# Graph layers on one core: the first group's preparation, weight sums and stage order rearranged

## The chip, the cores and the metric

The kernel runs on one core of a Trainium2 chip. The metric is the device time of one execution in microseconds (us), the median of several; smaller is better. A core has TensorE (PE in the profile, with PEld its weight loads), VectorE (DVE), ScalarE (ACT), GpSimd (POOL) and SyncE (SP, which here only issues DMAs). Each engine runs its own queue in order and waits on semaphores.

## The reference, cut to what matters

128 graphs of 64 nodes, 512 features each, go through four layers; each adds its input and is followed by a normalisation over the features (in the kernel `layer_norm`, without gain and offset).

```python
# layer 0, hypergraph convolution twice (H = adj != 0, w = first row of adj)
D = where(H @ w > 0, 1 / (H @ w), 0);  B = where(H.sum(0) > 0, 1 / H.sum(0), 0)
conv(x, W, b) = D * (H @ (B * (H.T @ (x @ W.T)))) + b
x = norm(x + conv(layer_norm(relu(conv(x, W1, b1)), gamma, beta), W2, b2) + x)
# layer 1: s = x @ w @ a; A = exp(leaky(8 tanh((s_i + s_j) / 8))) * adj, rows scaled to adj's row sums
x = norm(x + (A @ x) @ w)
# layer 2: three graph convolutions, relu after the first two
x = norm(x + adj @ (relu(adj @ (relu(adj @ x @ gW1 + gb1)) @ gW2 + gb2)) @ gW3 + gb3)
# layer 3: attention of 8 heads of 64, softmax mixed with exp(-adj) and adj, then Wout
x = norm(x + attention(x) @ Wout + bout)
```

## The kernel before, in words

All is float32. The 128 graphs are cut into 16 groups of 8 graphs (`T` = 512 rows, four tiles of 128 rows with two graphs each). A group passes through `first_half` (layers 0 and 1; stages named `a.`), `second_half` up to `dots` (layer 2, queries, keys, scores; `b.`), and the rest of it (softmax, values, output; `t.`). In one step of the main loop group q is in `a`, group q-1 in `b`, group q-2 in `t`. A string `order` in the code interleaves their stages; since PE runs its queue in order, a stage of one group fills PE while another group's stage waits for DVE or ACT. In step 0 there is only `a` of group 0, and nothing to fill with. The Tile framework's scheduler sets the final order of each engine's queue from the program's order and its own estimates; `tc.issue_after(i)` keeps what is emitted under it behind instruction i.

**Products.** `multiply` makes a 512x512x512 product from seven products of halves (`product`, L391) instead of eight: the left operand needs four sums on DVE (`Left.sums`, L370 to L373: s1 to s4), the right one four sums t1 to t4 of the weight's quarters. The seven products are called B11, T1, T2, B21, T3, B22, T4 in the order in which PE takes them; each is 8 records of 128x256 in the profile (16 for w2, whose left side has two halves). B11, T2, T3 and T4 build up in one PSUM tile, which is snapped in between (u1 after B11, u2 after T2), so the next of them waits for the eviction; T1 and B22 share another (u5 after T1). Graph products (`graph_T`, L340) use 64x64 matrices. All stages' PSUM copies are on ACT or DVE.

**Weights.** `Stream` keeps a ring of 20 tiles of 256 KB. A weight's first use loads its quarters, and `Weight.make` (L200 to L222) makes t1 to t4 on DVE when the stage takes it (L209 to L212) and writes them to HBM through SP (L218); later groups load all seven parts. W2 is first scaled by gamma on DVE (L207), and `beta_times` (L224) makes bw = beta @ W2.T on PE (L232) from w2's tiles, after c2 of group 0.

**Prepare.** `prepare` (L452 to L502) reads adj twice, by columns (`atc`) and by rows (`adn`), and its first row spread over the partitions (`wb`). It makes ht, hn (the two 0/1 matrices), hn*wb, the row sums deg, D and rowsum, B from ht; `inv` holds 1/D and 1/B, and through dg, hb, rbps (L486) and sps (L498) comes the matrix smat = H' B H D' (L501) that both graph products of layer 0 use. cs = inv * deg goes into the residual with bw (`constant`, L650).

**Order of group 0.** `prepare`, c1 (graph product of x with smat), w1a and w1b (the halves of W1), lnh (relu, LayerNorm of h), c2a and c2b (graph product of h), bw, w2 and the norm of x, then wa = w @ a (`make_wa`, L284: DVE products, sums, one matmul L299), s = x . wa (xwa, L605), e (L609), ss (L613: sums s over PE), t (tanh, exp, times atc), den (L626), its reciprocal rd (L631), c3 (graph product, L340), the l1 product with w, and the norm. `load` and `prep` of the next group stand behind a.c2b and b.k1. `prepare_masks` (L505) loads the masks and makes neg and adt at the end of stage agg.

Of the kernel before, what the change touches and what calls it, by code (L numbers as in the profile page):

```python
# [14 lines left out]
P = 128  # L15
# [25 lines left out]
def kernel(  # L41
# [61 lines left out]

    def load_group(q):


        g0 = q * 2 * G
        atc = grp.tile([P, G, C], FP, name=f"atc_{q}", tag="atc", bufs=3)
        nc.sync.dma_start(out=atc, in_=adjT[g0 : g0 + 2 * G].rearrange("(p g) e i -> (g e) p i", g=2))
        adn = grp.tile([P, G, C], FP, name=f"adn_{q}", tag="adn", bufs=2)  # L110
        nc.sync.dma_start(out=adn, in_=adj[g0 : g0 + 2 * G].rearrange("(p g) i e -> (g i) p e", g=2))
        wb = grp.tile([P, G, C], FP, name=f"wb_{q}", tag="wb", bufs=1)
        for h in range(2):
            nc.sync.dma_start(
                out=wb[h * C : (h + 1) * C],
                in_=adj[g0 : g0 + 2 * G, 0, :].rearrange("(p g) e -> g p e", g=2)[h].partition_broadcast(C),
            )
        xg = xp.tile([P, G, D], FP, name=f"x_{q}", tag="x")
        nc.sync.dma_start(
            out=xg, in_=x[q * T : (q + 1) * T, :].rearrange("(p t) d -> t p d", t=P)  # L120
        )
        atx = grp.tile([P, 2, C], FP, name=f"atx_{q}", tag="atx", bufs=3)
        for h in range(2):
            nc.sync.dma_start(
                out=atx[h * C : (h + 1) * C],
                in_=adjT[g0 : g0 + 2 * G].rearrange("(a z) e i -> z e a i", z=4)[1 + h],
            )
        return dict(q=q, atc=atc, atx=atx, adn=adn, wb=wb, x=xg)
# [37 lines left out]
    class Weight:  # L166
# [30 lines left out]
        def make(self, quads):  # L197

            got = [[None] * self.halves for _ in range(7)]
            if self.scaled:  # L200
                beta_times(quads)
            for u, b in enumerate(quads):
                if self.scaled:
                    for (k, n), t in b.items():
                        c0 = (u * 2 + k) * 2
                        g2 = ga_col[:, c0 : c0 + 2].unsqueeze(2).to_broadcast([P, 2, Q])
                        nc.vector.tensor_mul(t, t, g2)  # L207
                t1, t2, t3, t4 = (self.tile(f"t{n}", 0, u) for n in range(1, 5))
                nc.vector.tensor_sub(t1, b[0, 1], b[0, 0])  # L209
                nc.vector.tensor_sub(t2, b[1, 1], t1)  # L210
                nc.vector.tensor_sub(t3, b[1, 1], b[0, 1])
                nc.vector.tensor_sub(t4, b[1, 0], t2)  # L212
# [3 lines left out]
                for what, t in (whole | made if self.scaled else made).items():  # L216
                    kept[what] = dram.tile([P, 2, Q], FP, name=f"{self.name}k{what}_{u}", tag=f"{self.name}k{what}_{u}")
                    nc.sync.dma_start(out=kept[what], in_=t)  # L218
                self.kept.append(kept)
                for what, t in (whole | made).items():  # L220
                    got[what][u] = t
            return got  # L222

    def beta_times(quads):  # L224

        bb = sp.tile([P, DH // P, P], FP, name="bb", tag="s")
        nc.vector.tensor_copy(bb, be_col.unsqueeze(2).to_broadcast([P, DH // P, P]))
        ps = ps_gt.tile([P, 2, Q], FP, name="bwps", tag="gt")
        for n in range(2):
            for c in range(DH // P):  # L230
                u, k, kc = c // 4, c // 2 % 2, c % 2
                nc.tensor.matmul(  # L232
                    ps[:, n, :], bb[:, c, :], quads[u][k, n][:, kc, :],
                    start=(c == 0 and n == 0), stop=(c == DH // P - 1), skip_group_check=True,
                )
        nc.scalar.copy(bw_bc, ps.rearrange("p n f -> p (n f)"))
# [8 lines left out]
    class Stream:  # L245
# [12 lines left out]
        def pump(self):  # L258
            while self.todo and self.held + self.todo[0][3] <= RING:
                wt, q, what, n = self.todo.pop(0)  # L260
                if q == 0:
                    got = wt.load_quads()
                else:
                    got = [wt.load(q, what, u) for u in range(wt.halves)]
                self.here[wt, q, what] = got
                self.held += n

        def take(self, wt, q, what):
# [3 lines left out]
            if (wt, q, None) in self.here:  # L272
                self.here[wt, q] = wt.make(self.here.pop((wt, q, None)))
# [10 lines left out]
    def make_wa():  # L284

        a_bc = work.tile([P, D], FP, name="a_bc", tag="w")
        nc.gpsimd.dma_start(out=a_bc, in_=a.partition_broadcast(P))
        wa_col = small.tile([P, KD], FP, name="wa_col", tag="wa_col", bufs=1)
        for c in range(KD):
            wr = work.tile([P, D], FP, name=f"wr_{c}", tag="w")  # L290
            nc.sync.dma_start(out=wr, in_=w[c * P : (c + 1) * P, :])
            prod = work.tile([P, D], FP, name=f"waprod_{c}", tag="w")
            nc.vector.tensor_mul(prod, wr, a_bc)
            nc.vector.reduce_sum(wa_col[:, c : c + 1], prod, axis=AX.X)
        dg = work.tile([P, KD, P], FP, name="wa_diag", tag="w")
        for c in range(KD):
            nc.vector.tensor_scalar_mul(dg[:, c, :], ident, wa_col[:, c : c + 1])
        ps = ps_gt.tile([P, D], FP, name="wa_ps", tag="gt")
# [99 lines left out]
    def multiply(lefts, wt_q, dst, key, flipped=False, res=None, before=None, stops=(3,)):  # L398
# [14 lines left out]
        if before is not None:  # L413
            before()
# [37 lines left out]
    def prepare(g):  # L452
        q, atc, adn, wb = g["q"], g["atc"], g["adn"], g["wb"]

        ht = grp.tile([P, G, C], FP, name=f"ht_{q}", tag="ht", bufs=1)
        nc.vector.tensor_scalar(ht, atc, 0.0, None, ALU.not_equal)
        hn = grp.tile([P, 2, G, C], FP, name=f"hn_{q}", tag="hn", bufs=1)
# [507 lines left out]
```

## Time and profile before

| | us |
|---|---|
| median of 3 runs | 2870.9 (2870.55 to 2875.74) |
| the profiled execution | 2871.8 |
| its span (first to last instruction) | 2869.9 |
| PE busy in the span | 2773.6 (97%) |
| DVE busy | 2042.4 (71%) |
| ACT busy | 811.7 (28%) |
| POOL busy | 7.9 |

The profile is of one execution. Its page gives each engine's busy time, 40 slices of the span, DMA queues, the chain of work that ended last, and the costliest groups of instructions. Asked in detail, the trace gives the busy time by stretches of time, the waits (who waited for whom, total us, times, longest us), and a timeline (start us, duration us, engine, line, operation, out<-in). Durations of pipelined matmuls overlap: products of 8 records show 1.89 us and follow each other every 1.725 us.

### The profile page before, as it was taken

How to read it: one execution, taken by the hardware profiler on the slowest of the kernel's cores; microseconds unless marked ns; L12 is line 12 of the kernel's file. 1: busy time of each engine (PE TensorE's matmuls, PEld its weight loads, DVE VectorE, ACT ScalarE, POOL GpSimd, SP SyncE). 2: the span in 40 equal slices, each digit the busy share in tenths (PEclk: the TensorE clock that was granted, in tenths of full speed). 3: DMA queues.
4: the chain of work that ended last, by engine and by line, in shares of the span. 5: the costliest groups of instructions: out<-in, count | busy, mean ns of one | idle time of the engine just before them, and what ended most of it. 6: DMA issues, size and time to landing. Idle time of an engine off the chain costs nothing.

```text
span 2869.9 us, 67654 instructions
## 1 busy us (share of the span) xinstructions
PE 2773.6 (97%) x28802; PEld 2361.6 (82%) x28802; DVE 2042.4 (71%) x3933; ACT 811.7 (28%) x1444; POOL 7.9 (0%) x17
## 2 busy tenths in 40 slices
PE   5799999999999999999999999999999999999998
PEld 4677888888888888888888888888888888888876
DVE  6677767677686776867677686776767677676756
ACT  2132232323223232232323232232223323232222
POOL 1000000000000000000000000000000000000000
PEclk8899999999999999999999999999999999999999
DMA  6444545454454544545455454544545445454441
GB/s 187 162 125 122 152 128 166 127 156 141 131 167 130 161 128 136 165 126 162 127 147 153 128 163 132 156 127 136 166 129 154 128 139 156 126 162 130 146 119 63
DMA packets 313627, 406.05 MB, mean 141 GB/s; under 512 B 57936, under 2 KB 185456, under 8 KB 313328
## 3 DMA queue, kind: packets, MB, share of 16 engines
q1 hardware_dynamic: 312672, 400.13, 46.8%
q8 instruction: 228, 3.74, 0.5%
q0 software_dynamic: 656, 1.60, 0.2%
q14 instruction: 71, 0.58, 0.1%
HBM read 370.70 MB, written 30.93 MB: 140 GB/s over the span
## 4 chain that ended last, share of the span: by engine, by line
PE 80%; DVE 8%; ACT 3%; issue 0%; DVEq 0%; ACTq 0%
PE a_l0w L391 14%; PE b_l0w L391 7%; PE a_v L391 4%; PE a_k L391 4%; PE a_l2b L391 4%; PE a_l2c L391 4%; PE a_q L391 4%; PE a_l2a L391 4%; PE c_l0w L391 4%; PE a_wo L391 3%; PE gt_l L340 3%; PE gt_l0h L340 2%; PE a_l1w L391 2%; PE b_v L391 2%; PE b_k L391 2%; PE b_l2c L391 2%
## 5 line engine op out<-in xcount | busy, mean ns | idle before, releaser
L322 DVE BATCH_NORM_STATS2 st_l<-x 128x6 f32<-128x512 f32 x256 | 165.2, 672 | 0.6
L391 PE MATMUL a_l0w<-w2w,aT_l0h 128*128 128x256 f32 x720 | 164.3, 381 | 0.0
L391 PEld LDWEIGHTS a_l0w<-w2w,aT_l0h 128*128 128x128 f32 x720 | 135.6, 190 | 18.8
L562 ACT ACTIVATE h<-h 128x1024 f32<-128x1024 f32 x64 | 67.7, 1057 | 263.4 <-DVE h L432 239.2
L313 ACT ACTIVATE rs_l<-mv_l,eps_t 128x4 f32<-128x4 f32 x64 | 19.1, 298 | 373.9 <-DVE mv_l L323 373.9
L326 DVE TENSOR_SCALAR x<-x,mv_l,rs_l 128x512 f32<-128x512 f32 x256 | 122.5, 542 | 2.2
L348 ACT COPY aT_l<-gt_l 128x512 f32<-128x512 f32 x192 | 99.1, 598 | 86.9 <-PE gt_l L340 86.8
L391 PE MATMUL b_l0w<-w2w,s_l0h 128*128 128x256 f32 x480 | 108.5, 379 | 0.0
L391 PEld LDWEIGHTS b_l0w<-w2w,s_l0h 128*128 128x128 f32 x480 | 91.2, 190 | 12.4
L391 PE MATMUL a_wo<-wow,aT_oT 128*128 128x256 f32 x360 | 86.7, 384 | 8.5 <-DVE x L428 8.5
L698 ACT ACTIVATE aT_h<-gth,gb_col 128x256 f32<-128x256 f32 x128 | 48.5, 490 | 159.0 <-PE gth L690 159.0
L391 PE MATMUL a_l2b<-gwbw,aT_h 128*128 128x256 f32 x360 | 86.9, 384 | 4.7 <-ACT aT_oT L869 4.7
L408 DVE TENSOR_TENSOR u_l0w<-a_l0w,b_bc 128x512 f32<-128x512 f32 x64 | 43.9, 686 | 64.4 <-PE a_l0w L391 64.4
L391 PE MATMUL a_l1w<-ww,aT_l 128*128 128x256 f32 x360 | 86.9, 384 | 1.6
L391 PE MATMUL a_l0w<-w1aw,aT_l 128*128 128x256 f32 x360 | 88.2, 388 | 0.0
L391 PE MATMUL a_l2a<-aT_l,gwaw 128*128 128x256 f32 x360 | 86.6, 383 | 1.0 <-ACT aT_l L348 1.0
L391 PE MATMUL a_l0w<-w1bw,aT_l 128*128 128x256 f32 x360 | 87.3, 379 | 0.0
L391 PE MATMUL a_v<-wvw,aT_xT 128*128 128x256 f32 x360 | 86.6, 383 | 0.0
L391 PEld LDWEIGHTS a_wo<-wow,aT_oT 128*128 128x128 f32 x360 | 67.1, 190 | 23.0 <-DVE x L428 14.2
L391 PE MATMUL a_l2c<-gwcw,aT_h 128*128 128x256 f32 x360 | 86.0, 382 | 0.0
L391 PE MATMUL a_q<-aT_xT,wqw 128*128 128x256 f32 x360 | 85.1, 379 | 0.5 <-ACT aT_xT L737 0.5
L391 PE MATMUL a_k<-aT_xT,wkw 128*128 128x256 f32 x360 | 85.0, 379 | 0.0
(455 smaller groups left out, 6416.6 us busy)
## 6 DMA issues: line engine op xcount, KB each, us to landing
w2w<-w2k SPq DMA_DIRECT2D x210, 256.0 KB, 2.7
x<-in_x_dram SPq DMA_DIRECT2D x16, 1024.0 KB, 6.3
out_dram<-x SPq DMA_DIRECT2D x16, 1024.0 KB, 4.8
w1aw<-w1ak SPq DMA_DIRECT2D x60, 256.0 KB, 2.8
w1bw<-w1bk SPq DMA_DIRECT2D x60, 256.0 KB, 2.7
ww<-wk SPq DMA_DIRECT2D x60, 256.0 KB, 2.7
gwaw<-gwak SPq DMA_DIRECT2D x60, 256.0 KB, 3.8
gwbw<-gwbk SPq DMA_DIRECT2D x60, 256.0 KB, 2.7
```

What stands on the lines that cost most here:

```text
L313: nc.scalar.activation(rs, mv[:, :, 1], AF.Sqrt, bias=eps_t)
L322: nc.vector.bn_stats(st, xg[:, p, :])
L326: nc.vector.tensor_scalar(xg[:, p, :], xg[:, p, :], mv[:, p, 0:1], rs[:, p : p + 1], ALU.subtract, ALU.mult)
L340: nc.tensor.matmul(ps[g][f * C : (f + 1) * C, c, p, :], src(2 * duo + p)[rows, c0 : c0 + C], mat[rows, 2 * duo + p, :], start=True, stop=True,
L348: nc.scalar.copy(o[:, :, :, g, :], ps[g])
L391: nc.tensor.matmul(acc[:, blk, :], lhsT, rhs, start=(first and blk == 0 and i == 0), stop=(last and i == n_k - 1), skip_group_check=True,)
L408: nc.vector.tensor_add(t, ps, res(m, n))
L562: nc.scalar.activation(hn, hn, AF.Relu)
L698: nc.scalar.activation(o[:, :, h, :], ps[h][:, c].rearrange("p (d a) i -> p d (a i)", d=2), AF.Relu, bias=gb2_col[:, k : k + 1],)
```

## The change

- **Prepare of group 0.** D comes from 8 pairs of 64x64-by-64x1 products on PE (ht times the first column of atc) instead of adn, wb and DVE sums, and is copied from PSUM. `wb` is not loaded for group 0, deg and rowsum are made later. `prepare` becomes a generator in three parts: row work on DVE ("rows"), the rest ("prep"), for group 0 also the row sums.
- **Loads at the start.** x of group 0 in two halves, one on ACT's queue, ahead of adn; atx and masks of all groups with the group's loads (masks before: at agg); W2's raw quarters, w's rows, and all of group 1's inputs early.
- **Weights.** t1 to t4 of w1a stay on DVE; those of w1b, w2, w, gW1 to gW3, Wq, Wk, Wv and Wout are made on GpSimd, as soon as the ring lets them be loaded, and all writes to HBM are issued by GpSimd. W2 is loaded raw into two tiles of `big`, scaled by gamma on ACT into two others. bw is made from the raw tiles.
- **wa.** Its rows are loaded early, products and sums are one DVE operation per row block; its DVE part is emitted during w1b, its matmul behind bw's.
- **Order.** A string `start` is walked first, with each stage's PE work kept in turn: bw and wa between lnh and c2a; rows, prep and c1 of group 1 inside group 0's w2; group 1's w1a from w2's end to den, its residual, and its w1b and lnh behind the l1 product. The main order follows from step 1 without what is done, with "rows" for the next group behind a.w2 and "prep" where it was.
- **VectorE.** The residual of group 0 (2x + b2 and the bw term, `residual`) is emitted in turn behind lnh; later groups' rows behind w2's last add but one; `prepare_masks` behind the l2b product, with gb3.

In the built program the sequence of PE's stages in groups 2 to 15 is that of before. DVE's queue there differs in two places: the 11 kinds of row operations (ht, db, hn, rowsum, deg, hn*wb, db, gt, inv, dg, hb, cs) stand between w2's adds and t instead of beside the k product, and the five mask operations stand between gb3's adds and the eight sums for w2. Of GpSimd's 44 sums the program has four for each of nine weights and eight for w2.

```diff
+    def in_turn(*engines):
+        stack = ExitStack()
+        for e in engines:
+            stack.enter_context(tc.issue_after(
+                next(i for i in reversed(nc.cur_bb.bb.instructions) if i.engine == e)
+            ))
+        return stack
...
     def load_group(q):
...
+        xg = xp.tile([P, G, D], FP, name=f"x_{q}", tag="x")
+        xsrc = x[q * T : (q + 1) * T, :].rearrange("(p t) d -> t p d", t=P)
+        if q == 0:
+            nc.scalar.dma_start(out=xg[:, 0:2], in_=xsrc[:, 0:2])
         atc = grp.tile([P, G, C], FP, name=f"atc_{q}", tag="atc", bufs=3)
         nc.sync.dma_start(out=atc, in_=adjT[g0 : g0 + 2 * G].rearrange("(p g) e i -> (g e) p i", g=2))
+        if q == 0:
+            nc.sync.dma_start(out=xg[:, 2:4], in_=xsrc[:, 2:4])
         adn = grp.tile([P, G, C], FP, name=f"adn_{q}", tag="adn", bufs=2)
...
-        def make(self, quads):
+        def make(self, quads, engine):
...
-            if self.scaled:
-                beta_times(quads)
+            to_keep = []
             for u, b in enumerate(quads):
-                if self.scaled:
-                    for (k, n), t in b.items():
...
+                engine.tensor_sub(t1, b[0, 1], b[0, 0])
+                engine.tensor_sub(t2, b[1, 1], t1)
+                engine.tensor_sub(t3, b[1, 1], b[0, 1])
+                engine.tensor_sub(t4, b[1, 0], t2)
...
+            with in_turn(POOL):
+                for k, t in to_keep:
+                    nc.gpsimd.dma_start(out=k, in_=t)
             return got
...
+        def load_raw(self):
+            self.raw = []
+            for u in range(self.halves):
+                t = big.tile([P, 4, 2, Q], FP, name=f"{self.name}r_{u}", tag="big")
+                for n, (k, m) in enumerate(((0, 0), (0, 1), (1, 1), (1, 0))):
+                    nc.sync.dma_start(out=t[:, n], in_=self.quad_src(u, k, m))
+                self.raw.append(t)
+        def scale(self):
+            quads = []
+            for u, raw in enumerate(self.raw):
+                s = big.tile([P, 4, 2, Q], FP, name=f"{self.name}s_{u}", tag="big")
+                b = {}
+                for n, (k, m) in enumerate(((0, 0), (0, 1), (1, 1), (1, 0))):
+                    for c in range(2):
+                        f = (u * 2 + k) * 2 + c
+                        nc.scalar.mul(s[:, n, c], raw[:, n, c], ga_col[:, f : f + 1])
+                    b[k, m] = s[:, n]
+                quads.append(b)
+            return quads
+        def beta_times(self):
+            bb = sp.tile([P, DH // P, P], FP, name="bb", tag="s")
+            nc.gpsimd.tensor_copy(bb, be_col.unsqueeze(2).to_broadcast([P, DH // P, P]))
+            ps = ps_gt.tile([P, 2, Q], FP, name="bwps", tag="gt")
+            for n in range(2):
+                for c in range(DH // P):
+                    u, k, kc = c // 4, c // 2 % 2, c % 2
+                    nc.tensor.matmul(
+                        ps[:, n, :], bb[:, c, :], self.raw[u][:, ((0, 1), (3, 2))[k][n], kc, :],
+                        start=(c == 0 and n == 0), stop=(c == DH // P - 1), skip_group_check=True,
+                    )
+            nc.scalar.copy(bw_bc, ps.rearrange("p n f -> p (n f)"))
...
         def pump(self):
             while self.todo and self.held + self.todo[0][3] <= RING:
                 wt, q, what, n = self.todo.pop(0)
-                if q == 0:
-                    got = wt.load_quads()
+                self.held += n
+                if q > 0:
+                    self.here[wt, q, what] = [wt.load(q, what, u) for u in range(wt.halves)]
+                elif wt is w_1[0]:
+                    quads = wt.load_quads()
+                    with in_turn(DVE):
+                        self.here[wt, q] = wt.make(quads, nc.vector)
                 else:
-                    got = [wt.load(q, what, u) for u in range(wt.halves)]
-                self.here[wt, q, what] = got
-                self.held += n
+                    self.here[wt, q] = wt.make(wt.scale() if wt.scaled else wt.load_quads(), nc.gpsimd)
...
+    def make_wa(a_bc, wr):
         wa_col = small.tile([P, KD], FP, name="wa_col", tag="wa_col", bufs=1)
         for c in range(KD):
-            wr = work.tile([P, D], FP, name=f"wr_{c}", tag="w")
-            nc.sync.dma_start(out=wr, in_=w[c * P : (c + 1) * P, :])
-            prod = work.tile([P, D], FP, name=f"waprod_{c}", tag="w")
-            nc.vector.tensor_mul(prod, wr, a_bc)
-            nc.vector.reduce_sum(wa_col[:, c : c + 1], prod, axis=AX.X)
+            nc.vector.scalar_tensor_tensor(
+                wr[c], wr[c], 1.0, a_bc, ALU.mult, ALU.mult, accum_out=wa_col[:, c : c + 1]
+            )
         dg = work.tile([P, KD, P], FP, name="wa_diag", tag="w")
         for c in range(KD):
             nc.vector.tensor_scalar_mul(dg[:, c, :], ident, wa_col[:, c : c + 1])
+        return dg
+    def spread_wa(dg):
...
     def prepare(g):
-        q, atc, adn, wb = g["q"], g["atc"], g["adn"], g["wb"]
+        q, atc, adn = g["q"], g["atc"], g["adn"]
...
+        def by_rows():
+            nc.vector.tensor_scalar(hn[:, 0], adn, 0.0, None, ALU.not_equal)
+            nc.vector.reduce_sum(deg, hn[:, 0], axis=AX.X)
+            nc.vector.reduce_sum(rowsum, adn, axis=AX.X)
+        if q == 0:
+            d_ps = [ps_gt.tile([P, G], FP, name=f"dps_{q}_{h}", tag="gt") for h in range(2)]
+            for p in range(G):
+                for h in range(2):
+                    rows = slice(h * C, (h + 1) * C)
+                    nc.tensor.matmul(
+                        d_ps[h][rows, p : p + 1], ht[rows, p, :], atc[rows, p, 0:1], start=True, stop=True
+                    )
+            for h in range(2):
+                rows = slice(h * C, (h + 1) * C)
+                nc.vector.tensor_copy(db[rows, 0], d_ps[h][rows])
+        else:
+            by_rows()
+            nc.vector.tensor_mul(hn[:, 1], hn[:, 0], g["wb"])
+            nc.vector.reduce_sum(db[:, 0], hn[:, 1], axis=AX.X)
...
         nc.vector.tensor_mul(hb, ht, bcast(inv[:, 1], G))
+        yield
...
+        if q == 0:
+            yield
+            by_rows()
+        nc.vector.tensor_mul(cs, inv[:, 0], deg)
+        yield
...
-                with behind(f"l0w10_{q}"):
-                    for p in range(G):
-                        nc.vector.scalar_tensor_tensor(xg[:, p, :], xg[:, p, :], 2.0, b2_bc, ALU.mult, ALU.add)
-                    if q > 0:
-                        constant(g)
+                if q > 0:
+                    with behind(f"l0w10_{q}"):
+                        residual(g)
                 yield "resid"
...
+        if q == 0:
+            with in_turn(DVE):
+                residual(g)
         for left in lefts:
             left.sums()
         yield "c2b"
-        gen = multiply(lefts, (w_2, q), nat(xg), f"l0w2_{q}", res=nat(xg), before=(lambda: constant(g)) if q == 0 else None)
...
-    def constant(g):
+    def residual(g):
         for p in range(G):
+            nc.vector.scalar_tensor_tensor(
+                g["x"][:, p, :], g["x"][:, p, :], 2.0, b2_bc, ALU.mult, ALU.add
+            )
             nc.vector.scalar_tensor_tensor(
                 g["x"][:, p, :], bw_bc, g["cs"][:, p : p + 1], g["x"][:, p, :], ALU.mult, ALU.add
             )
...
         with behind(f"l2b_{q}"):
             for p in range(G):
                 nc.vector.tensor_add(xg[:, p, :], xg[:, p, :], gb3_bc)
+            prepare_masks(g)
         yield "gb3"
...
         layer_norm(xg, f"l2_{q}")
-        prepare_masks(g)
         yield "agg"
...
+    start = """
+        a0.c1 a0.w1a1 a0.w1a rows0 a0.resid a0.w1b1 wa a0.w1b a0.lnh bw a0.c2a a0.c2b rows1 a0.w21 prep1 a1.c1 a0.w2
+        a1.w1a1 a1.w1a2 a0.ss a1.w1a a1.resid a0.den a0.c3 a0.p1 a0.p2 a1.w1b1 a1.w1b a1.lnh
+    """.split()
     order = """
         t.v1 a.c1 t.v b.gt t.soft a.w1a1 a.w1a t.soft2 a.resid b.l2a1 b.l2a a.w1b1 t.ptp a.w1b t.pv a.lnh t.osum
-        b.l2b1 a.c2a b.l2b a.c2b b.gb3 load a.w21 b.gh a.w2 b.l2c1 b.l2c2 a.ss b.l2c t.o1 a.den t.o2 a.c3 b.agg t.o a.p1 b.xT
-        a.p2 b.q1 b.q t.ln3 b.k1 prep b.k b.dots
+        b.l2b1 a.c2a b.l2b a.c2b b.gb3 load a.w21 b.gh a.w2 rows b.l2c1 b.l2c2 a.ss b.l2c t.o1 a.den t.o2 a.c3 b.agg t.o
+        a.p1 b.xT a.p2 b.q1 b.q t.ln3 b.k1 prep b.k b.dots
     """.split()
...
+    stream = Stream([(used[who, name], q) for who, q, name in todo if (who, name) in used])
+    groups, gens, preps = {0: first}, {}, {0: prepare(first)}
+    next(preps[0])
+    next(preps[0])
+    stream.pump()
+    with in_turn(SP):
+        w_2.load_raw()
+        wa_parts = load_wa()
+    with in_turn(SP):
+        load_atx(first)
+        load_masks(first)
+        groups[1] = load_group(1)
+    for n, (who, q, name) in enumerate(todo):
+        with in_turn(PE) if n < len(start) else nullcontext():
+            if who == "load":
+                if q > 1:
+                    groups[q] = load_group(q)
+            elif who == "rows":
+                if q > 0:
+                    preps[q] = prepare(groups[q])
+                with behind(f"l0w2_{q - 1}") if q > 1 else in_turn(DVE):
+                    next(preps[q])
+            elif who == "prep":
+                next(preps[q])
+            elif who == "wa":
+                with in_turn(DVE):
+                    wa_parts = make_wa(*wa_parts)
+            elif who == "bw":
+                w_2.beta_times()
+                spread_wa(wa_parts)
```

## The prediction

> **What bounds the kernel now.** First I read the page's totals and its 40 slices: TensorE (PE) is busy in 97% of the span, and what it lacks is nearly all in the first three slices and the last.
>
> ```profile
> PE   5799999999999999999999999999999999999998
> PEclk8899999999999999999999999999999999999999
> ```
>
> The table by stretches of 20 us says how much (PE's busy time is the second number, the granted clock comes after POOL):
>
> ```profile
> 0.00:20.00 20.00, 6.36 (x147) 5.43 (x147) 8.46 (x29) 3.17 (x6) 7.37 (x16) 1.00 0.81 239
> 20.00:40.00 20.00, 18.01 (x80) 14.95 (x80) 15.68 (x28) 3.16 (x4) 0.54 (x1) 1.00 0.89 296
> 40.00:60.00 20.00, 11.44 (x166) 9.68 (x167) 18.04 (x54) 4.95 (x7) 0.00 (x0) 0.78 0.43 122
> 60.00:80.00 20.00, 10.11 (x155) 8.66 (x152) 10.49 (x20) 3.13 (x6) 0.00 (x0) 0.62 0.16 49
> 100.00:120.00 20.00, 9.23 (x36) 6.49 (x34) 14.73 (x36) 2.17 (x3) 0.00 (x0) 0.81 0.53 182
> 120.00:140.00 20.00, 14.14 (x167) 11.67 (x168) 6.89 (x12) 5.01 (x10) 0.00 (x0) 0.67 0.12 31
> 140.00:160.00 20.00, 14.93 (x310) 13.13 (x309) 17.65 (x45) 6.46 (x11) 0.00 (x0) 0.91 0.24 74
> ```
>
> With the 0.13 us of 80 to 100 that is 55.9 us of idle PE in 160 us, where the first group runs alone. From 380 to 2780 PE is busy for 2380.0 of 2400 us, so there nothing can be won, but anything that delays PE is lost. The waits of PE name what ends each gap:
>
> ```profile
> PE rbps L486 <- DVE dg L482: 12.9, 1, 12.9
> PE bwps L232 <- issue: 9.9, 1, 9.9
> PE wa_ps L299 <- DVE wa_diag L297: 8.0, 1, 8.0
> PE gt_l0h L340 <- DVE h L579: 7.5, 1, 7.5
> PE gt_l L340 <- DVE smat L501: 4.6, 1, 4.6
> PE ss L613 <- DVE e L609: 5.1, 2, 3.8
> ```
>
> All but bwps wait for VectorE (DVE), and bwps is behind it too: its operand bb stands in DVE's queue after a wait of 6.9 us for wb of a later group. The two waits for ss, 5.1 us in all, are in the first two groups. In later groups e is just in time, which matters below:
>
> ```profile
> 929.21 1.89 PE L391 MATMUL a_l2c<-gwcw,s_h 128*128 128x256 f32 x8
> 930.39 0.41 DVE L609 TENSOR_TENSOR e<-identc,s 128x256 f32<-128x256 f32 x1
> 930.93 0.62 PE L613 MATMUL ss<-e,bones 128*128 128x256 f32 x2
> ```
>
> Products of 8 records start every 1.725 us, so the one before ss gives way at 930.93, 0.13 us after e ends. There is no slack at this point.
>
> **Part 1: up to the second group's w2.** Both kernels have done the same PE work when w2 of group 1 begins (212.22 us in before), so I walk the changed queues up to there, with before's durations.
> - D by TensorE. Before, the wait for wb (DVE 6.85 to 9.57) and the chain after it put dg's end at 12.82. Now: atc lands at 3.06 as before, ht 0.29, the small products as sps (1.12), two copies and six small operations of 0.2, then hb, identc and dg (1.06): 7.3 us. So everything after is 5.5 us earlier; c1 starts at 10.4 (15.91 before). x was issued at 3.19 behind wb and landed at 15.9; now both halves are issued by 2 us, with half of it on ACT's queue. At the 169 GB/s of 5 to 10 us and 294 after, the 1.7 MB up to x are there by about 9, and the first two tiles of w1a by about 12.3. My value is that x does not gate.
> - w1a: B11 4 us after c1 as before (14.4), T1 at 16.5, seven products 12.1, 0.7 for the cold clock, 1.4 of waits for evictions: ends at 28.3 (34.67 before). w1b: 12.1, and 2.1 because eight operations of wa (3.4 us) stand ahead of T3's eviction: 42.5 (48.57 before).
> - The LayerNorm of h left PE idle 7.5 us; now bw stands there (32 records of 0.216: 6.9; before it took 10.04 at a lower clock) and wa_ps (0.9): c2 at 50.3 (56.1 before). With bw out of the way behind c2, w2 starts at 55.3 (82.25 before). Its sums t1 to t4 are no longer in DVE's queue.
> - w2: 24.2, with prep and c1 of group 1 inside (1.25 + 2.3) and two waits for DVE (u1 behind eight sums and seven row operations 1.2, smat 1.0): 85.2. Before 107.2, without those two stages.
> - Then the new order leaves gaps. The scheduled DVE queue has u1 of group 1's w1a behind group 0's LayerNorm and xwa (8.0 us after w2), where PE has B11 and T1 for 3.4: 5.0 idle. den 1.4; w1a, ss and den 13.3, cold clock 0.5: den ends at 105.4. Between den and c3 stand h's add, four bn_stats, six operations of the residual and the 1.76 reciprocal: 8.5 idle, against 2.4 before: c3 at 113.9. From c3 to the end of the l1 product it takes 16.5 as before: 130.4.
> - w1b of group 1: 12.1 + 1.65 behind LayerNorm l1: 144.1. Now b.gt (2.1) and l2a, which before had w1a to hide behind: idle 3.6 until LN h and s1 are done; before l2b 1.6 more for ReLU and s1. With l2a, l2b (12.1 each) and c2 (4.2) w2 of group 1 starts at 179.8.
> Gain: 212.2 - 179.8 = **32.4 us**.
>
> **Part 2: what the new engines cost.** GpSimd makes 44 sums (w1b 4, w2 8, eight weights of 4) and issues 54 writes that SP had. No GpSimd tensor operation of this size is in the trace; the nearest row is the affine select, 0.30 us for 128x128, so four times that, 1.2 us, is my estimate for 128x512; below it the 0.69 of DVE's own row, and above it twice my value, 2.4. With 0.54 per issue (the rows of its loads) a weight takes 7.0 us, 11.8 at the top, against 12.1 of PE per product stage. So the sums are hidden, and ACT's 16 scalings (0.42 each by the row of adt) too: 6.7 us on an engine busy for 28%. Their ring slots come free a stage ahead by the order of uses. What remains is whether GpSimd slows DVE. Nothing in before runs on both. Low end 0. For the high end I take ten of the sums falling where the walk has DVE on the path (wa, LN l1, sums), 1.2 us each: 12. I take 5, nearer the low end, since most of DVE's operations there read PSUM.
>
> [...]
>
> **Part 3: every later group.** PE's order does not change, but DVE's does. The row part of prepare (ht, db, hn, rowsum, deg, hn*wb, then db, gt, inv, dg, hb, cs) is moved from beside b.k, where nothing waited, to just after w2's last adds, in the chain to e and t. Before e six operations are added, by start-to-start spacings 0.2 + 0.33 + 0.2 + 0.33 + 0.33 + 0.33 = 1.72; g's add (0.6) moves behind e; 0.7 of them fits in gaps (0.1 after x's add, 0.35 while ACT makes the square root, the rest while bn_aggr drains). e is late by 0.41, and PE with it, as it has no slack. Behind e another nine operations stand ahead of t, but tanh waits until 933.03 for a table load anyway and den had 0.5 to spare with ss late: no further loss. 13 groups (2 to 14) x 0.41 = **5.3**; ends 0 and 0.9 x 13 = 12. In group 1 the six inv operations stand ahead of e as well, and g: 2.3 more.
>
> The masks (5 operations, 1.5 us) move ahead of the eight sums for w2. Before, DVE idles 0.84 there, so the sums start 0.7 later; the T1 product needs s1 of the second half 0.9 after it does now, and u1 for T2 then has 0.0 left. 2 for 15 groups, ends 0 and 4. Their loads, and those of adn, atc and wb, are issued a stage or more ahead on SP; SP loses 54 writes of about 0.33 and gains nothing that waits. The tail keeps its order: 0.
>
> **Sum.** 32.4 - 5 - 2.3 - 5.3 - 2 = 17.8. The profiled execution took 2871.8 (span 2869.9 and 1.9 around it): 2854.0. The median shown is 0.9 lower: **2853**.
>
> **Rivals.**
> - The new waits cost nothing: PE's scheduled order absorbs the 0.41, GpSimd and DVE don't meet. For it: the trace shows 1.0 to 2.5 us of idle DVE between evictions nearby. Against it: the ss row. 2871.8 - 32.4 + 1 (left for group 1) - 0.9 = 2839.5.
> - The gain is eaten: every cost at its high end, 12 + 12 + 4 + 2.3 = 30.3 of 32.4, so 2868.5. In effect the change does not do what it says: PE waits as long, elsewhere. For it: DVE is 71 to 75% busy and the moved work sits on its tightest chain.
> - Slower, one mechanism: the row operations in the chain to ss. If none of them overlaps ACT's waits, each group loses 1.72 before e and 1.5 before t (db, gt, three inv and their waits), 3.2 x 13 = 42, and the time is 2871.8 - 32.4 + 5 + 2.3 + 42 + 2 - 0.9 = 2890. It decides from (32.4 - 9.3) / 13 = 1.8 us per group. Against it: tanh's table load and the square root's wait are in the trace, and six of the operations need nothing of that chain.
>
> **Chances.** Forecast (2842 to 2863) 0.46; free 0.22; eaten 0.20, of which 0.08 below 2865; slower 0.12. What a measurement of this kernel can tell from no change is about 0.2%, 5.7 us: faster below 2865.2 is 0.46 + 0.22 + 0.08 = 0.76, the same 0.12, slower 0.12. The range, 2830 to 2870, takes in the free case and nearly all of the eaten one, and leaves the slower one out.
>
> **What would show it.** dg's end near 7 us and c1 near 10.5; bwps right behind w1b, with no 10 us gap; w2 of group 0 starting at 55 and of group 1 near 180; PE gaps of about 5 and 8.5 us at u1 of group 1's w1a and at c3; DVE's 128x512 operations not longer than 0.69 before 200 us; about 0.4 us of idle PE at ss in groups 2 to 14. I would be wrong if x or w1 landed after 13 us, if GpSimd's sums took over 2.4 us, or if ss waited over 1 us in each group.

## The result and the profile after

The change is slower: 2882.5 us (median; 2880.8 to 2883.3) against 2870.6 (2868.9 to 2875.7) for the kernel before on the same chip, a ratio of 1.0037 [1.0026, 1.0049], so by 0.4%. The forecast was 2853. The profiled execution took 2880.8, with a span of 2878.7 (2869.9 before).

The slices and the first four stretches of 20 us of the kernel after, with the columns as in the prediction (length, then busy us of PE, PEld, DVE, ACT, POOL, then granted clock, DMA share, GB/s):

```profile
PE   7788999999999999999999999999999999999998
PEclk9899999999999999999999999999999999999999
```

```profile
0.00:20.00 20.00, 10.49 (x174) 8.76 (x175) 8.63 (x29) 4.22 (x7) 10.34 (x22) 1.00 0.95 267
20.00:40.00 20.00, 16.40 (x60) 13.04 (x59) 11.28 (x16) 6.69 (x14) 12.57 (x13) 0.83 0.78 271
40.00:60.00 20.00, 17.73 (x73) 14.49 (x73) 15.38 (x35) 5.76 (x10) 14.05 (x19) 0.91 0.83 282
60.00:80.00 20.00, 16.45 (x302) 13.79 (x301) 15.41 (x28) 5.38 (x10) 4.05 (x3) 0.91 0.54 191
```

The start did fill up: over the eight stretches PE is idle for 37.9 of the first 160 us, against 55.9. But POOL, hardly used before past 20 us, is busy for 10 to 14 of 20 us in the first three, and the clock is below full in 20 to 80 (0.83, 0.91 and 0.91; before 1.00, 0.78 and 0.62). The clock's records start at 16.6 us, so the 1.00 of the first row says little: c1 takes 4.23 us there and 2.09 in later groups. From 200 to 415 us, where before lost 4.6 us of PE, after loses 13.3. The waits of PE up to 200 us, and from 200 to 415 (total, times, longest):

```profile
PE a_l0w L463 <- DVE u_l0w L480: 11.0, 4, 4.4
PE gt_l L412 <- DVE t L714: 7.6, 1, 7.6
PE gt_l0h L412 <- issue: 3.0, 1, 3.0
```

```profile
PE a_q L463 <- DVE qT L498: 3.6, 1, 3.6
PE ss L695 <- DVE e L691: 3.5, 1, 3.5
PE b_l0w L463 <- DVE s_l0h L442: 3.3, 1, 3.3
```

The waits for wb's chain, bwps and wa_ps are gone. The longest wait of the first row (4.4, at 108.7 us) and the second row are the new gaps that the prediction had priced (5.0 and 8.5). In the second list, the wait for e of group 1 was 1.3 before, and the prediction had put 2.3 on top of it; qT (0.4 before) and s_l0h are in no step of it. In a steady step, where e was just in time (... stands for lines left out):

```profile
932.47 1.89 PE L463 MATMUL a_l2c<-gwcw,s_h 128*128 128x256 f32 x8
...
933.61 0.42 DVE L553 TENSOR_TENSOR hn<-hn,wb 128x256 f32<-128x256 f32 x1
933.95 0.42 DVE L691 TENSOR_TENSOR e<-identc,s 128x256 f32<-128x256 f32 x1
...
934.42 0.70 PE L695 MATMUL ss<-e,bones 128*128 128x256 f32 x2
```

A row operation (hn*wb) stands right ahead of e, and ss starts 1.95 after the product ahead of it instead of 1.72: 0.23 late. From one ss to the next a step takes 173.22 (172.64 before), so 0.58 are lost in each; the other 0.34 is lost between ss and den, which are 6.03 apart instead of 5.69.

**Where it went**, by milestones (us from the start; e2 is the experiment with the sums back on DVE):

| | before | forecast | after | e2 |
|---|---|---|---|---|
| c1 starts | 15.9 | 10.4 | 11.8 | 12.2 |
| w1a of group 0 ends | 34.7 | 28.3 | 37.0 | 37.3 |
| w1b ends | 48.6 | 42.5 | 53.1 | 52.0 |
| w2 of group 0 starts | 82.5 | 55.3 | 70.2 | 65.1 |
| l1 product of group 0 ends | - | 130.4 | 147.6 | 140.2 |
| w2 of group 1 starts | 212.2 | 179.8 | 199.3 | 190.0 |
| ss of group 2 | 413.0 | - | 414.7 | 390.4 |

The new order is worth 22 us at w2 of group 1 (e2), not 32; with the sums on GpSimd 13 are left there, and none at ss of group 2. What GpSimd and DVE do to each other, first DVE, then POOL (start, duration), at the sums behind the 3.3 us wait:

```profile
201.89 0.69 DVE L442 TENSOR_TENSOR s_l0h<-aT_l0h 128x512 f32<-128x512 f32 x1
202.61 1.64 DVE L443 TENSOR_TENSOR s_l0h<-s_l0h,aT_l0h 128x512 f32<-128x512 f32 x1
204.17 1.74 DVE L444 TENSOR_TENSOR aT_l0h<-aT_l0h 128x512 f32<-128x512 f32 x1
205.84 0.68 DVE L445 TENSOR_TENSOR s_l0h<-aT_l0h,s_l0h 128x512 f32<-128x512 f32 x1
```

```profile
202.22 1.48 POOL L246 TENSOR_TENSOR gwct<-gwcb,gwcb 128x512 f32<-128x512 f32 x1 [3.07 <-PE a_l0w L463]
203.78 1.59 POOL L247 TENSOR_TENSOR gwct<-gwcb,gwct 128x512 f32<-128x512 f32 x1
```

The two DVE operations that start while a GpSimd sum runs take 1.64 and 1.74 and end 0.55 us after it, as if they had begun only when it was through; the one that started before it and the one after it take 0.69 and 0.68. The GpSimd sums, 1.27 alone, stretch as well. Small operations lose most for their size (128x8: 0.17 to 1.13), and a TENSOR_SCALAR with one SBUF input was held too (128x256: 0.28 to 1.01). Not held up beside such a sum were DVE's evictions from PSUM (0.69), its reductions (0.41) and BATCH_NORM_STATS (0.68).

### The profile page after: what moved, and what is told of

It is laid out like the page before. It is cut to its first block, busy times and chain, and to the rows that moved or that the text cites. A ratio compares the mean times of both kernels' runs of the same rounds, so it can differ in the third digit from the quotient of the medians.

```text
span 2878.7 us, 67727 instructions
## 1 busy us (share of the span) xinstructions
PE 2787.9 (97%) x28818; PEld 2365.4 (82%) x28818; DVE 2016.3 (70%) x3880; ACT 816.7 (28%) x1460; POOL 98.6 (3%) x116
## 4 chain that ended last, share of the span: by engine, by line
PE 76%; DVE 18%; ACT 3%; DMA 1%; issue 1%; SPq 0%; DVEq 0%; ACTq 0%
PE a_l0w L463 13%; PE b_l0w L463 7%; PE a_l2b L463 4%; PE c_l0w L463 4%; PE a_k L463 4%; PE a_v L463 4%; PE a_l2a L463 4%; PE a_q L463 4%; PE gt_l L412 3%; DVE st_l L394 3%; PE a_wo L463 2%; PE a_l1w L463 2%; PE gt_l0h L412 2%; PE b_l2a L463 2%; PE b_v L463 2%; PE b_l2b L463 2%
## 5 line engine op out<-in xcount | busy, mean ns | idle before, releaser
L480 DVE TENSOR_TENSOR u_l0w<-a_l0w,b_bc 128x512 f32<-128x512 f32 x64 | 43.9, 687 | 64.1 <-PE a_l0w L463 64.0
```

What stands on the lines that cost most here:

```text
L480: nc.vector.tensor_add(t, ps, res(m, n))
```

## Experiments

Theories: **A**, GpSimd's sums exclude DVE's operations and cost most of the miss; **B**, the row operations in the chain to ss do (the prediction's slower rival); **C**, the start's loads are late. Times are medians; the ratio is to the kernel before.

**e1, the row operations back beside b.k** (the order string "a.w2 rows ... b.k1 prep b.k" becomes "a.w2 ... b.k1 rows prep b.k", without an anchor).

> The changed kernel (2882.5 us) with the row operations of groups 2 to 15 back beside the k product; group 1's stay in the start. Theory 'rows in the chain': the changed kernel's steps are 173.22 us apart where those of before are 172.64, 0.58 more, because e and t come late behind the row operations. Undone, the steps are 172.64 again (13 x 0.58 = 7.5 us), and the wait of 3.46 us for e in the first full step gets shorter too (2 to 4 us with the clock behind it): 2871 to 2875. Rival 'masks': the 0.58 comes from the mask operations ahead of the sums for w2; then the steps stay near 173.2 and the time at 2879 to 2882.

Measured: 2888.1, 1.0063 [1.0050, 1.0076]; slower than the change itself. Half of the steps do return to 172.65, so the 0.58 is the rows' alone and the masks cost nothing. But other steps take 173.0 to 175.2, with waits of PE named "issue" (up to 2.0), and without the anchor the scheduler spread groups 1 and 2's row work over the start (w2 of group 1 at 206.3). Theory B's price is confirmed at 0.58 x 13 = 7.5 us, too little to be the miss; the edit moved more than the rows, so its total (2871 to 2875 expected) says nothing.

**e2, the sums back on DVE.** GpSimd keeps the writes; all weights but w1a get their sums when the stage takes them:

```diff
 # in pump
+    self.here[wt, q, None] = wt.scale() if wt.scaled else wt.load_quads()
 # in take
+    if (wt, q, None) in self.here:
+        self.here[wt, q] = wt.make(self.here.pop((wt, q, None)), nc.vector)
```

> The changed kernel with the sums of all weights on VectorE, made when a stage takes its weight; GpSimd keeps the writes. Theory 'exclusion': 19.5 us of DVE's time in the first 300 us is lost because a DVE operation that meets a GpSimd sum takes 1.75 instead of 0.69 us, and PE waits for a good half of it, each time followed by a stretch at half clock. Without the GpSimd sums PE's wait of 2.82 us at T2 of w1a, of 3.31 at w2 of group 1 and of 3.57 at the q product go, although DVE gets 40 sums (27 us) more: w2 of group 1 starts at 188 to 194 instead of 199.3, the time is 2866 to 2873. Rival 'DVE is short of time': the 27 us of sums cost PE more than the exclusion did: w2 of group 1 no earlier than 199, 2883 to 2892.

Measured: 2858.5, 0.9960 [0.9948, 0.9973], 24 us below the change although DVE makes the 44 sums (30 us; the expectations count 40) itself. That is more than the 9.5 to 16.5 expected, with w2 of group 1 at 190.0 as expected. The waits of 3.5 for e and 3.6 for qT shrink to these:

```profile
PE ss L699 <- DVE e L695: 1.8, 1, 1.8
PE a_q L467 <- DVE qT L502: 0.6, 1, 0.6
```

This speaks for A; the step stays at 173.21, as B says. Up to ss of group 2, 24.3 us earlier here, PE was idle for 12.7 us more in the changed kernel and busy for 11.6 more: it worked for 36.2 us at half clock there and for 11.8 here. So half of what GpSimd cost came through PE's clock.

**e3, each GpSimd sum in four pieces of 128x128** (the same elements and engine, shorter operations): `for c in range(2): for j in cut: engine.tensor_sub(out[:, c, j], ...)`.

> The changed kernel with each GpSimd sum of 128x512 cut into four of 128x128; the same bytes on the same engine at about the same total time (1.2 to 1.5 us per sum). Theory 'exclusion for a whole instruction': a DVE operation then waits for at most one piece, 0.3 to 0.4 us, instead of 1.06; the lost DVE time in the first 300 us falls from 19.5 to 6 to 10 us, no DVE operation of 0.69 takes over 1.2, and the time falls by 3 to 8 us to 2875 to 2880. Rival 'shared bandwidth': both engines go at a lower rate while both are busy; then the lost time stays at 17 to 21 us and the time at 2881 to 2884.

Measured: 2870.2, 1.0001 [0.9992, 1.0010]; 12.3 below the change, more than forecast. The sums of the same tile, two that met pieces:

```profile
198.70 0.94 DVE L448 TENSOR_TENSOR aT_l0h<-aT_l0h 128x512 f32<-128x512 f32 x1
199.56 0.94 DVE L449 TENSOR_TENSOR s_l0h<-aT_l0h,s_l0h 128x512 f32<-128x512 f32 x1
```

0.94 instead of 1.74: such an operation now waits for one piece. With the same bytes moved, bandwidth shared between the two would have left it as it was; exclusion by instruction fits. Two things fit less well: the DVE time lost in the first 300 us (each operation against the usual time of its form) fell from about 20 to about 14 us, not to 6 to 10, as more operations are held, each for less; and one operation found no way between the pieces, a product for wa at 40.90 that took 4.08 instead of 0.69 while w2's pieces ran one behind the other.

**e10, idle sums.** e2, and in `make` four GpSimd sums per weight half into a tile nobody reads (44 in all), so that nothing can wait for a late sum.

> The kernel of e2 with 40 GpSimd sums added that nobody reads: four for each weight from its quarters (eight for w2), written to a scratch tile when the stage takes the weight. Theory 'exclusion': what cost time in the changed kernel is that VectorE stands still while a GpSimd sum runs; then sums that nobody waits for cost as well: 10 to 25 us above 2858.5, with VectorE's operations with two SBUF operands again up to 1.75 us. Rival 'late sums': the cost came from products that wait for t1 to t4 from the slower engine; then idle sums cost nothing: within 2 us of 2858.5.

Measured: 2886.6, 1.0058 [1.0044, 1.0072], 28.1 above e2. DVE, then POOL (4 in a row):

```profile
243.39 0.41 DVE L699 TENSOR_TENSOR e<-identc,s 128x256 f32<-128x256 f32 x1
243.72 1.49 DVE L576 TENSOR_TENSOR dg<-identc,inv 128x256 f32<-128x256 f32 x1
...
246.54 1.22 DVE L602 TENSOR_TENSOR cs<-inv,deg 128x4 f32<-128x4 f32 x1
```

```profile
243.56 5.53 POOL L251 TENSOR_TENSOR idle_wq<-wqb,wqb 128x512 f32<-128x512 f32 x4 [8.97 <-DVE g L504]
```

Even a 128x4 operation takes 1.22. This settles A: sums that nobody waits for cost as much, so the loss is the exclusion and not weights that come late. The scratch tiles share a ring with other work tiles, but no wait in the trace ends on one of them. DVE's operations lost about 18 us in the first 300, the time grew by 28.1. What DVE's loss leaves out is PE's clock: up to ss of group 2, e10 is 29.1 behind e2, with PE idle for 21.1 more and busy for 8.0 more (33.8 us of its work at half clock against 11.8). In the change itself, right after the 3.5 us wait for e, PE (second number) gets half the clock (0.50) for 3.3 us:

```profile
242.00:245.30 3.30, 3.30 (x9) 2.59 (x8) 0.69 (x3) 0.42 (x1) 0.00 (x0) 0.50 0.22 78
```

**e4, the "issue" gap of 3.0 at c2.** The idea was that PE's instructions wait behind the data of W2's writes, which this edit holds back until c2 is through: a 128x1 GpSimd copy that reads c2's last result, ahead of W2's writes.

> The changed kernel with the 14 writes of w2's parts (3.6 MB) held back until c2 of group 0 is through, by one 128x1 copy on GpSimd that reads c2's last result. Theory 'code behind data': PE's gap of 3.04 us within c2, which no wait in the trace explains, ends when 16 KB of instructions land at 65 to 66 us, behind data that fills the DMA engines from 55 to 68 us at about 400 GB/s. With the writes held the gap is under 1 us, w2 starts at 66 to 68 instead of 70.2, and the time falls by 2 to 5 us to 2877 to 2880. Rival: the gap is not from the DMA traffic; it stays near 3 us and the time within 1 us of 2882.5.

Measured: 2880.2, 1.0036 [1.0023, 1.0050]. The gap stays (2.74; the writes start at 64.7, behind its end at 61.2), so it isn't these writes; the time, near the range expected, says nothing for the theory. The gap stands ahead of the last 93 of c2's small 64x64 products and has 2.5 to 3.2 us in most runs, 0.55 in e2. The last section has what the traces show of it.

**e5, rows behind the scores, and e9, rows in DVE's idle slot.** Both are e2 with the rows elsewhere: e5 `"b.q1 b.q rows t.ln3"` behind q's last eviction, e9 `"b.agg t.o rows a.p1"` behind the output product's, where DVE waits 5.03 us for ACT.

> The kernel of e2 (all sums on VectorE, 2858.5 us) with the row operations of groups 2 to 15 behind the q product's last add but one, in a fixed place, where e1 had let the scheduler choose. Theory 'rows in the chain': the steps go from 173.21 back to 172.64 us (13 x 0.57 = 7.4) and group 1's wait for e of 1.8 us goes: 2849 to 2852. Rival 'loads': the loads of adn and wb wait for the tiles that the row operations free, so they come later and meet the load of x and the instruction fetches, as in e1, where single steps were 0.4 to 2.5 us longer; then the gain is eaten: 2855 to 2862.

> The kernel of e2 (2858.5 us) with the row operations of groups 2 to 15 behind the output product's last adds, where VectorE waits 5.03 us for the transposed x in every step; they take about 4.6 us there. In e5 they stood ahead of the normalisation that frees x's buffer, so the next group's x came late and c1 waited for it. Theory 'chain and loads': the place counts in two ways, ahead of e and t it delays PE by 0.57 us a step, ahead of the normalisation of x it delays the load of x. Here it does neither: steps of 172.64 us, no wait for x, 2849 to 2852. Rival: the freed tiles let the loads of adn and wb fall on another busy stretch, or s1 to s4 of the transposed x come late: steps of 173 or more, 2856 to 2864.

e5: 2880.2, 1.0032 [1.0020, 1.0045], 21.7 above e2 and missed. e9: 2852.3, 0.9937 [0.9925, 0.9950], 6.2 below e2, at the upper end of what was expected, with the step at 172.65. PE's waits in e5 (total, times, longest) and SP's issue of the next x in e5 (ss of that step at 565.9) and in e9 (at 565.6):

```profile
PE gt_l L416 <- DMA x<-in_x_dram: 8.4, 11, 1.9
```

```profile
629.99 0.37 SPq L139 DMA_DIRECT2D x<-in_x_dram  x1
```

```profile
624.58 0.38 SPq L139 DMA_DIRECT2D x<-in_x_dram  x1
```

In e5 the rows delay the last norm, hence the output's transfer, hence the buffer of x: x is issued 64.1 after ss instead of 59.0, and c1, 68.8 after it, waits for x. These waits are 8.4 of the 21.7; three "issue" gaps within c1 (6.5) and waits for dg and sm (3.9), none of which e2 has, make up most of the rest. So a place with idle DVE isn't enough; what stands behind it must not release a transfer. e9's slot, and the same place in e2:

```profile
936.77 0.41 DVE L541 TENSOR_REDUCE rowsum<-adn 128x4 f32<-128x256 f32 x1
...
940.98 0.69 DVE L446 TENSOR_TENSOR s_xT<-aT_xT 128x512 f32<-128x512 f32 x1 [0.90 <-ACT aT_xT L827]
```

```profile
940.79 0.69 DVE L446 TENSOR_TENSOR s_xT<-aT_xT 128x512 f32<-128x512 f32 x1 [5.03 <-ACT aT_xT L827]
```

The idle time ahead of s_xT shrinks from 5.03 to 0.90, and s_xT starts no later in its step (30.1 us behind ss, 30.4 in e2).

**e6, w1b's sums behind u2 of w1a** (e2 with `in_turn(DVE)` around w1b's `make` at a.w1a1; W2's eight sums on GpSimd again), **e7** = e5 + e6, **e11** = e9 + e6.

> The kernel of e2 with the four sums of w1b behind u2 of w1a, where VectorE is idle for 3.9 us, instead of ahead of s1 to s4 of group 0, and the eight sums of w2 on GpSimd again. Theory: in e2 T1 waits 3.42 us for s1 behind the sums of w1b, and half clock follows for 6.8 us; without that w1a ends at 31 to 33 us instead of 37.3, and w2's GpSimd sums (36 to 46 us) meet little of VectorE's work with two SBUF operands: w2 of group 0 starts at 59 to 62 instead of 65.1, the time is 2852 to 2855. Rival: GpSimd's w2 sums cost more on VectorE than they save there: 2857 to 2861.

> e5 and e6 together. If both theories hold the gains add up: 2858.5 - 7.4 - 1.8 - 5 = 2843 to 2847. If they share a wait: 2848 to 2852.

> e9 and e6 together (w1b's sums behind u2 of w1a, w2's sums on GpSimd). If the two add up 1.6 us below e9: 2847 to 2851. If GpSimd's w2 sums cost what they spare: the same as e9 within 1.5 us.

e6: 2856.9, 0.9952 [0.9938, 0.9965]; 1.6 below e2, within the intervals, and short of the 2852 to 2855 expected. w1a ends at 33.3 (37.3 in e2), but the c2 gap is back to 3.1 us and w2 starts only 0.6 earlier. e7: 2879.8, 1.0030 [1.0019, 1.0042]: e5's wait for x again; missed with it. e11, as expected: **2849.3**, 0.9927 [0.9915, 0.9940].

**e8, e12, e13, the first loads (C).** e8 is e7 with x wholly on SP behind atc and with adn behind W2's and w's loads; e12 is e11 with that order and the biases' row loads (768 KB) later; e13 is e12 with adn behind w1b's quarters.

> e7 with the first loads in the order atc, x, w1a, all on SP, and adn behind w2 and w. Theory: atc lands at 4.9 us in the changed kernel instead of 3.1 since x's first half goes beside it; and w1a's quarters land at 15.5 and 16.4, which holds up s1 to s4 behind w1a's sums. With the new order ht is 1.5 us earlier, w1a's sums 1 to 2 us earlier, and the time 1 to 3 us below e7. Rival: x gates c1 then (x lands after 10 us), and the time is the same as e7's or up to 2 us above.

> e11 with less traffic ahead of w1a: atc, x and w1a in this order on SP, adn behind w2 and w, and the rows of b2, gb3 and bout (768 KB as spread over the partitions) behind the writes of w1a on GpSimd. Theory 'w1a gates': c1 was on time in e8 (10.0 us, 10.4 predicted) but T1 waited for s1 behind w1a's sums, whose quarters land at 15.3 to 16.4 us. 768 KB at the 246 GB/s of the first 16 us are 3.1 us; w1a's sums then begin at 12 to 13.5, T1 at 16 to 17.5 instead of 18.8, and the time is 2 to 5 us below e11. Rival: w1a's landing is set by its own queue and not by the traffic beside it: sums from 15 us on, time as e11 within 1.5 us.

> e12 with adn right behind w1b's quarters on SP. In e12 w1a went as the theory 'w1a gates' has it (T1 at 16.7 instead of 19.7 us in e11, w1a's end at 31.5 instead of 33.8), but adn, put behind w2 and w, landed at 36.8, and hn, which stands ahead of u1 of w1b in VectorE's queue, held up T2 by 4.46 us with half clock behind it. With adn landed before 31 us that wait goes: w1b starts at 31.5 and ends at 45 to 46, the time is 2845 to 2848, 2 to 4 us below e11 (2849.3). Rival: what w1a gains is lost again before w2, at the gap of 3 us within c2 that no wait explains, or in the clock; then 2849 to 2851.

e8: 2878.7, 1.0029 [1.0018, 1.0040], no clear gain on e7. ht starts at 3.03 and c1 at 10.0, as the prediction had it, but w1a's sums still wait for its quarters (15.3). e12: 2853.9, 0.9941 [0.9929, 0.9954]: the sums start at 13.3, T1 at 16.7 (16.5 predicted) and w1a ends at 31.5, but the time is above e11's, where 2 to 5 below were expected: adn lands at 36.8 and hn, ahead of u1 in DVE's queue, waits 4.4 for it. e13: **2848.9**, 0.9919 [0.9905, 0.9933]: that wait is gone, yet w1a ends at 33.5 and the time is that of the rival. The T2 product in e12, then in e13, and the stretch behind it in each (clock after POOL):

```profile
20.83 1.99 PE L468 MATMUL a_l0w<-w1at,s_l 128*128 128x256 f32 x8 [2.15 <-DVE u_l0w L485]
...
22.00:25.30 3.30, 3.30 (x17) 2.90 (x16) 0.69 (x1) 0.00 (x0) 0.00 (x0) 1.00 0.99 233
```

```profile
21.13 2.83 PE L468 MATMUL a_l0w<-w1at,s_l 128*128 128x256 f32 x8 [2.16 <-DVE u_l0w L485]
...
22.10:25.30 3.20, 3.20 (x9) 2.54 (x8) 0.00 (x0) 0.00 (x0) 0.00 (x0) 0.50 1.00 249
```

The same gap of PE (2.15 and 2.16), the full clock in one, half of it in the other (the last section has what tells them apart). C explains the late start of w1a, but of what it gains there nothing is left at the end (e13 and e11 agree within their intervals). e2, e6, e9, e11, e12 and e13 beat both kernels, e11 and e13 by most, 0.7 to 0.8% below the kernel before.

## Why the prediction was wrong

The span was to shrink by 17.8 and grew by 8.8, a miss of 26.6. It divides so:

- **GpSimd, 19.3 of it. The step that failed** is in Part 2: "I take 5, nearer the low end, since most of DVE's operations there read PSUM". After against e2 at ss of group 2 is 24.3. The duration was right (1.2 estimated, 1.27 measured alone). The 5 itself was an estimate that no run shows, as nothing in before runs on both engines; the runs showed 24.3 in its place. Its reason holds in the changed kernel, where evictions from PSUM take 0.67 to 0.69 beside a sum too. What it missed: the operations that PE waits for are not mostly these. The sums s1 to s4, the residual, the row operations, e and t's product with atc have two operands in SBUF, stand one after another, and those that met a sum were held (the ones of 128x512 took up to 1.78 instead of 0.69); and gaps of PE were followed by half the clock (36.2 us of its work up to ss of group 2, 11.8 in e2), which this term left out, though the walk of the first group had the cold clock. Its high end of 12 is about what PE idled (12.7); the 11.6 of slower work behind the gaps was not in it. The 24.3 is a net figure: e2 makes the 44 sums on DVE.
- **The first group's walk, 10.2**, by w2 of group 1 in e2 (190.0 against 179.8). 9.0 of it is there when w1a ends: "ends at 28.3" was 37.3. x itself landed at 5.0 and 6.3. But atc landed at 4.9 instead of 3.06, with x's first half beside it (3.0 in e8, with x behind it), the first two quarters of w1a were there at 15.5 instead of 12.3 in the changed kernel (the last at 16.9), and s1 stands behind w1a's sums in DVE's queue. Not all of the 9.0 is the loads': in e2 the four sums of w1b (2.6 us) stand ahead of s1 as well, and without them (e6) w1a ends at 33.3; in the change, which ends at 37.0, these are on GpSimd instead, s3 and s4 take 1.78 and 1.75 beside them, and PE waits 2.8 for u1. Nor is one trace exact here: e9, with the same instructions up to 60 us as e2, has 35.0. The warning "if x or w1 landed after 13 us" was the one that came true. Behind w1a, the walk's 151.5 us to w2 of group 1 took 152.7, with bw at 7.1 (6.9 forecast) and the two new gaps at 5.6 and 8.1 (5.0 and 8.5).
- **From there to ss of group 2, -2.8**: e2 gains 0.4 there where a loss of 2.4 was forecast.
- **Part 3, -0.1**: from ss of group 2 on 7.1 lost, 7.2 forecast. The sum was right by luck, through errors that cancel: the rows cost 0.58 a step, not 0.41 (0.23 at ss, and 0.34 between ss and den, where "no further loss" stood), and the masks nothing, not 2 (e9: rows moved, masks left, step 172.65).

Three figures of the prediction are slightly off, which changes nothing: 14.4, 12.1, 0.7 and 1.4 give 28.6 and not 28.3, the sum for "eaten" gives 2868.8 and not 2868.5, and w2 of group 0 started at 82.46 before, not 82.25.

Of the rivals, the free one is out. By its number the result lies between "eaten" (2868.5) and "slower" (2890); by mechanism it is "eaten", beyond its high end. The slower rival's mechanism is there at a third of its size: it needed 1.8 a step, and 0.58 came. The chance of 0.12 for slower was too small because I gave the GpSimd conflict no case on that side: the high end took ten of the 44 sums at 1.2 us (12), while all 44 at the same estimate are 53, more than the gain of 32.

## What to carry to other kernels

Work moved from DVE to GpSimd isn't off DVE's path while it runs beside DVE operations with two SBUF operands (1.64 and 1.74 us here instead of 0.69); count those on the path, at about one GpSimd instruction each (1.27 alone), add PE's half clock behind the gaps that come of it (11.6 of the 24.3 us here), and keep the work on DVE (2858.5 here) rather than cut GpSimd's operations small (2870.2). When work has to leave a tight chain, look for a slot where the engine waits for another and where nothing behind it releases a buffer: the row operations cost 7.5 us (0.58 x 13) ahead of e, 21.7 more ahead of an output transfer, and next to nothing in the right gap (steps of 172.65 against 172.64). A forecast for a start-up phase needs the landing of every load in its new order, since a load issued beside the first one delayed it here (atc at 4.9 instead of 3.0).

## What was not expected of the hardware

- A GpSimd sum holds small DVE operations for as long as large ones (128x4: 0.15 to 1.22), and is itself stretched from 1.27 to up to 1.83. 44 sums that nobody reads cost 28.1 us.
- Behind a gap of 2.16 us PE's clock was half for about 3.4 us in one run, and behind one of 2.15 at the same place in another it was not. The traces tell them apart. In each of the 15 traces all changes of the clock lie a multiple of 3.41 us apart; cut the span into stretches at these points, and in the stretch that holds the gap PE is busy for 1.26 us (37%) in e13 (18.71 to 22.13) and for 1.46 (43%) in e12 (18.88 to 22.29). Over all traces, from the first record of the clock on, each of the 101 stretches at full clock with PE busy for 40% or less is followed by half the clock, none of the 12175 with over 53%, and 19 of the 47 between. So how a gap falls on these stretches counts beside its length.
- PE stalls 2.5 to 3.2 us within c2 in most runs with no wait shown, and holding W2's writes back didn't remove it. In all 14 traces of kernels with the new start the gap ends 1.3 to 1.6 us after a transfer of 16 KB has landed on the DMA queue that the page calls "instruction": it lands at 66.19 and the gap ends at 67.61 after, at 62.20 and 63.51 in e2. After, this transfer starts 0.65 us into the gap; in e2, whose gap is only 0.55, 2.0 us ahead of it. This fits a wait for instructions; no run changed it on purpose, so the cause isn't shown.
